# Position terms of the attention scores: one 120-row bfloat16 matmul per head, or two in the head's own half of the rows

## The chip, the core and the metric

The kernel runs on one core of a Trainium2 chip. Its metric is the device time of one launch in microseconds (us). A core has a matrix engine (TensorE, PE in the profile; its weight loads are a row of their own, PEld), a vector engine (DVE), an activation engine (ACT), a general engine (POOL, GpSimd) and a queue engine that issues most DMAs (SP). SBUF and PSUM have 128 partitions[...].

## What is computed

The whole program is a transformer block with attention, followed by three spectral and scan layers on a 48 x 48 grid of tokens with 768 channels. Only the attention matters here: 12 heads of 64 channels, T = 2304 queries and as many keys.

```python
attn = jnp.einsum('bqc,bkc->bqk', q * scale, k)
rel_h = jnp.einsum('bhwc,hkc->bhwk', r_q, Rh)
rel_w = jnp.einsum('bhwc,wkc->bhwk', r_q, Rw)
attn = (attn.reshape(B * nh, H, W, H, W) + rel_h[:, :, :, :, None] + rel_w[:, :, :, None, :]).reshape(B * nh, H * W, H * W)
attn = jax.nn.softmax(attn, axis=-1)
out = jnp.einsum('bqk,bkc->bqc', attn, v)
```

A score is thus the product of query and key plus two position terms: one depends on the query and the key's row of the grid, one on the query and the key's column.

## The kernel before

The qkv phase writes q, k, v to DRAM, and the position terms too: `rw_d` and `rh_d` hold, for each query and each head, 48 column terms and 48 row terms. Each float32 term is kept as a sum of three bfloat16 parts, so that three bfloat16 products with a 0/1 table give back the float32 value nearly whole.

`attention_bounded` then works on pairs of heads (6), chunks of 464 queries (5, the last of 448) and tiles of 128 keys (18). The tile's keys are 8 rows by 16 columns of the grid. A list `work` cuts the 18 key tiles of a chunk into items of KB = 3, which gives 6 x 5 x 6 = 180 items. The scores are kept transposed, keys on partitions and queries along the free dimension; a tile of both heads fills two PSUM banks, and there are three such buffers.

For each item the program issues, in this order:

- `products` (line 576) for the three key tiles: per head one float32 matmul of keys by queries. Head 0 has its 64 channels in partitions 0 to 63, head 1 in 64 to 127. The hardware's records show each float32 matmul as two, each with its own weight load.
- `scores` (line 585) for the same three tiles: per head one bfloat16 matmul that adds the position terms to the same PSUM tile. Its weights are a 0/1 table `oneh` of 120 rows; its moving operand `bt` has 120 rows for the head: 3 parts x 16 columns, and 3 parts x 24 rows of the grid. The 48 grid rows are cut into two halves of 24, and the key's columns into KJ = 3 groups of 16, so `bt` is held for 2 x 3 cases and both heads. Then comes the exponential on ACT (line 587) into a float32 tile `p`, and the sum over key tiles on DVE (lines 592 and 595).
- `values` (line 606) for the three tiles of the item before: per head one float32 matmul of 64 output columns, accumulated over the chunk. Behind a chunk's last scores come its `row_sums` (line 614), the reciprocal (line 616), and, after the values, the final product (line 622).

The engines run their instructions in program order; only SP's and POOL's side work is placed between them by the scheduler. Two sets of query and bias tiles alternate by chunk: `load_chunk` is called at the start of a chunk for the next one and calls `load_bias` once per head (lines 505 and 506, four DMAs per head and per segment; a chunk that crosses a multiple of 768 queries has two segments). The `p` tiles come from a pool of ten. The same pool serves as the gate of `weight_sums`, a side stream that, once every six items, loads blocks of the projection and MLP weights (lines 776 and 796), combines them on POOL (lines 131 to 142) and stores them back (lines 780 and 802). All its DMAs go through the SP queue too. `load_ahead` loads the first chunk and the 0/1 table during the qkv phase.

`attention_any` is a second branch for scores out of bounds. It doesn't run with these inputs.

Of the kernel before, what the change touches and what calls it, by code (L numbers as in the profile page):

```python
# [12 lines left out]
F32 = mybir.dt.float32  # L13
BF16 = mybir.dt.bfloat16
# [6 lines left out]
P = 128  # L21
# [5 lines left out]
NH, HD = 12, 64  # L27
FF = 4 * C
NF = FF // P
TB = 384  # L30
NTB = T // TB
QB = 464
NQB = -(-T // QB)
LN_EPS = 1e-5
KTH, KTW = 8, 16
KJ = G // KTW
NBR = 3 * (KTW + G // 2)
# [469 lines left out]
        at += m  # L507


def queries(qc):  # L510

    return slice(qc * QB, min(T, (qc + 1) * QB))


def load_onehot(nc, pool, oneh_d, o):

    f = pool.tile([P, 3, P], F32, tag="onehf", name="onehf")
    nc.sync.dma_start(f[:NBR], oneh_d)
    nc.vector.tensor_copy(o[:NBR], f[:NBR])


def attention_loads(nc, q_d, k_d, v_d, rw_d, rh_d):

    def keys_values(kv, pr):
        nc.sync.dma_start(kv[:, :T], k_d[pr * P : (pr + 1) * P, :])
        nc.sync.dma_start(kv[:, T:].rearrange("p (t c) -> p t c", t=NT), v_d[:, :, pr * P : (pr + 1) * P])

    def chunk(qb, c):  # L530
        pr, qc = c
        q = queries(qc)
        n = q.stop - q.start
        nc.sync.dma_start(qb[0][:, :n], q_d[pr * P : (pr + 1) * P, q])
        for s in range(2):
            load_bias(nc, qb[1][:, s, :, :, :n], rw_d, rh_d, 2 * pr + s, q.start, n)

    return keys_values, chunk


def attention_bounded(tc, ahead, oT, beside, load_next):

    nc = tc.nc
    KB = 3
    (load_keys_values, load_chunk), kvs, qbs, ones, oneh = ahead
    with (
        tc.tile_pool(name="at_p", bufs=10) as pp,
        tc.tile_pool(name="at_r", bufs=2) as rp,
        tc.tile_pool(name="at_o", bufs=2) as op,
        tc.tile_pool(name="at_ps", bufs=3, space=PSUM) as ps_s,  # L560
        tc.tile_pool(name="at_pv", bufs=1, space=PSUM) as ps_v,
    ):
        keys = [kv[:, :T] for kv in kvs]
        vals = [kv[:, T:].rearrange("p (t c) -> p t c", t=NT) for kv in kvs]

        probs, scs = {}, {}
        size = lambda c: queries(c[1]).stop - queries(c[1]).start
        held = lambda c: qbs[(c[0] * NQB + c[1]) % 2]

        def products(c, kt):  # L570
            pr, qc = c
            n = size(c)
            ps = ps_s.tile([P, 2, 512], F32, tag="s", name=f"s_{pr}_{qc}_{kt}")
            for s in range(2):
                rows = slice(s * HD, (s + 1) * HD)
                nc.tensor.matmul(ps[:, s, :n], lhsT=keys[pr % 2][rows, kt * P : (kt + 1) * P], rhs=held(c)[0][rows, :n], start=True, stop=False)  # L576
            scs[c, kt] = ps

        def scores(c, kt):
            pr, qc = c  # L580
            n = size(c)
            b, j = divmod(kt, KJ)
            ps = scs.pop((c, kt))
            for s in range(2):
                nc.tensor.matmul(ps[:, s, :n], lhsT=oneh[:NBR, b % 3, :], rhs=held(c)[1][:NBR, s, b // 3, j, :n], start=False, stop=True)  # L585
            p = pp.tile([P, 2, QB], F32, tag="p", name=f"p_{pr}_{qc}_{kt}")[:, :, :n]
            nc.scalar.activation(p, ps[:, :, :n], AF.Exp)  # L587
            probs[c, kt] = p

            if kt == 1:  # L590
                acc = rp.tile([P, 2, QB], F32, tag="acc", name=f"acc_{pr}_{qc}")[:, :, :n]
                nc.vector.tensor_tensor(acc, probs[c, 0], p, ALU.add)
                probs[c] = acc
            elif kt > 1:
                nc.vector.tensor_tensor(probs[c], probs[c], p, ALU.add)  # L595

        avs, recs = {}, {}

        def values(c, kt):
            pr, qc = c  # L600
            if kt == 0:
                avs[c] = ps_v.tile([P, 512], F32, tag="av", name=f"av_{pr}_{qc}")
            p = probs.pop((c, kt))
            for s in range(2):
                rows = slice(s * HD, (s + 1) * HD)
                nc.tensor.matmul(avs[c][rows, : size(c)], lhsT=vals[pr % 2][:, kt, rows], rhs=p[:, s, :], start=kt == 0, stop=kt == NT - 1)  # L606

        def row_sums(c):
            pr, qc = c
            n = size(c)  # L610
            acc = probs.pop(c)
            rs = ps_v.tile([P, 512], F32, tag="rs", name=f"rs_{pr}_{qc}")
            for s in range(2):
                nc.tensor.matmul(rs[s * HD : (s + 1) * HD, :n], lhsT=ones, rhs=acc[:, s, :], start=True, stop=True)  # L614
            rec = rp.tile([P, QB], F32, tag="rec", name=f"rec_{pr}_{qc}")[:, :n]
            nc.vector.reciprocal(rec, rs[:, :n])  # L616
            recs[c] = rec

        def finish(c):
            pr, qc = c  # L620
            av, rec = avs.pop(c), recs.pop(c)
            nc.vector.tensor_tensor(oT[:, pr, queries(qc)], av[:, : size(c)], rec, ALU.mult)

        work = [((pr, qc), k0) for pr in range(NC) for qc in range(NQB) for k0 in range(0, NT, KB)]
        other = beside(op, lambda name: pp.tile([P, 2, QB], F32, tag="p", name=name).rearrange("p a c -> p (a c)")[:, : 2 * TB].rearrange("p (a c) -> p a c", a=2))
        for i in range(len(work) + 1):
            if i % 6 == 3:
                next(other, None)
            if i == len(work) - 8:
                load_next()  # L630
            if i < len(work):
                c, k0 = work[i]
                pr, qc = c
                if k0 == 0:
                    nxt = (pr, qc + 1) if qc + 1 < NQB else (pr + 1, 0)
                    if nxt[0] < NC:
                        load_chunk(held(nxt), nxt)
                    if qc == 1 and pr + 1 < NC:
                        load_keys_values(kvs[(pr + 1) % 2], pr + 1)
                for kt in range(k0, k0 + KB):  # L640
                    products(c, kt)
                for kt in range(k0, k0 + KB):
                    scores(c, kt)
            if i:
                c, k0 = work[i - 1]
                if k0 + KB == NT:
                    row_sums(c)
                for kt in range(k0, k0 + KB):
                    values(c, kt)
                if k0 + KB == NT:  # L650
                    finish(c)
        for _ in other:
            pass


def attention_any(tc, ident, oneh, q_d, k_d, v_d, rw_d, rh_d, oT, beside, load_next):


    nc = tc.nc
# [6 lines left out]
    with (  # L666
# [7 lines left out]
    ):  # L674
        ones = cp.tile([1, HD], F32, tag="ones", name="an_ones")
        nc.vector.memset(ones, 1.0)
        ka = cp.tile([HD, T], F32, tag="ka", name="an_ka")
        vt = cp.tile([P, NT, HD + 1], F32, tag="vt", name="an_vt")
        nc.vector.memset(vt[:, :, HD : HD + 1], 1.0)
        for h in range(NH):  # L680
# [4 lines left out]
            bt = hp.tile([P, 2, KJ, T], BF16, tag="bt", name=f"an_bt_{h}")  # L685
            for i in range(NTB):
                load_bias(nc, bt[:, :, :, i * TB : (i + 1) * TB], rw_d, rh_d, h, i * TB, TB)
            for t in range(NT):
                s = sp.tile([P, T], F32, tag="s", name=f"an_s_{h}_{t}", bufs=1)
                m6 = sp.tile([P, T // TB], F32, tag="m6", name=f"an_m_{h}_{t}")  # L690
                for i in range(T // TB):
                    ps = ps_s.tile([P, 512], F32, tag="s", name=f"an_sp_{h}_{t}_{i}")
                    cols = slice(i * TB, (i + 1) * TB)
# [12 lines left out]
                for k0 in range(0, NT, 4):  # L706
                    n = min(4, NT - k0)
                    ps = ps_t.tile([P, 512], F32, tag="t", name=f"an_pt_{h}_{t}_{k0}")
                    for j in range(n):
                        k = k0 + j  # L710
# [600 lines left out]
def block_kernel(ctx: ExitStack, tc: tile.TileContext, a: dict):  # L1311
    nc = tc.nc
# [16 lines left out]
    loads = attention_loads(nc, q_d, k_d, v_d, rw_d, rh_d)  # L1329
    kvs, ahead = [], []  # L1330
    atc = at_stack.enter_context(tc.tile_pool(name="at_c", bufs=1, side="left"))
    oneh = atc.tile([P, 3, P], BF16, tag="oneh", name="oneh")

    def kv_tile():
        kvs.append(home.tile([P, 2 * T], F32, tag="xn", name=f"kv_{len(kvs)}"))

    def load_ahead(stage):
        if stage == 0:
            load_onehot(nc, atc, a["oneh"], oneh)
            kv_tile()  # L1340
            loads[0](kvs[0], 0)
            return
        kv_tile()
        pool = at_stack.enter_context(tc.tile_pool(name="at_a", bufs=1, side="left"))
        qbs = [(pool.tile([P, QB], F32, tag=f"qt{i}", name=f"qt{i}"), pool.tile([P, 2, 2, KJ, QB], BF16, tag=f"bt{i}", name=f"bt{i}")) for i in range(2)]
        loads[1](qbs[0], (0, 0))
        ones = pool.tile([P, HD], F32, tag="ones", name="ones")
        nc.vector.memset(ones, 1.0)
        ahead.extend((loads, kvs, qbs, ones, oneh))
# [16 lines left out]
    with tc.If(bounded > 0) as which:  # L1366
        attention_bounded(tc, ahead, oT, beside, load_pw)
    with which.Else():
        attention_any(tc, ident, oneh, q_d, k_d, v_d, rw_d, rh_d, oT, beside, load_pw)
    at_stack.close()  # L1370
    xr_d = dram.tile([T, C], F32, tag="xr_d", name="xr_d")
    proj_phase(tc, x, pw, ps_d, a["proj_b"], oT, xr_d)
# [484 lines left out]
```

## Time and profile before

| quantity | value |
|---|---|
| median of 3 runs | 3815.2 us (3811.54 to 3820.01) |
| the profiled execution's own time | 3815.61 us |
| its span, first to last instruction | 3813.4 us |
| attention, from its first product to the end of the last values | about 512 to 1666 us |
| mean granted clock of TensorE | 0.987 |
| bytes moved by DMA | 460.28 MB |

Median durations of the rows that the change concerns:

| line | instruction | count | ns of one |
|---|---|---|---|
| L576 | matmul, keys by queries, float32 | 2160 | 549 |
| L576 | weight load 64x128, float32 | 2160 | 187 |
| L585 | matmul, position terms, bfloat16 | 1080 | 359 |
| L585 | weight load 120x128, bfloat16 | 1080 | 98 |
| L587 | exponential, both heads | 540 | 940 (mean) |
| L595 | sum over key tiles | 480 | 1170 (mean) |
| L606 | matmul, probabilities by values, float32 | 2160 | 557 (mean) |

A matmul's duration in the profile runs from its start to its modelled end, and neighbours overlap; what one costs in a stream is the distance from one start to the next. In a line of the timeline the columns are start, length, engine, source line, operation, output and inputs, shapes and count; in square brackets stands idle time before it and what ended it.

### The profile page before, as it was taken

The page shows a single profiled execution, that of the slowest core. Times are in us where ns is not written, and L with a number is a line of the kernel's source. Part 1 is how long each engine was busy: PE and PEld are TensorE (multiplying, and loading weights), DVE is VectorE, ACT ScalarE, POOL GpSimd, SP SyncE. Part 2 cuts the span into 40 slices and gives each one's busy share as a digit, 9 for nine tenths or more (in the row PEclk, how much of TensorE's full clock was granted, in tenths as well). Part 3 has the DMA queues.
Part 4 walks back from the last instruction along what each step waited for, and adds up shares of the span by engine and source line. Part 5 has one row for each costly group of instructions (what it writes and reads, how often), then busy time and mean ns, then how long its engine had stood idle before and what let it go on. Part 6 is the DMA issues. An engine that isn't in the chain of part 4 may idle for free.

```text
span 3813.4 us, 51839 instructions
## 1 busy us (share of the span) xinstructions
PE 3707.4 (97%) x20914; PEld 2168.0 (57%) x20914; DVE 2032.0 (53%) x3070; ACT 1135.3 (30%) x1803; POOL 653.5 (17%) x498
## 2 busy tenths in 40 slices
PE   7999979999999999998999999999999998999998
PEld 4666543333333333345555555555568876996685
DVE  6655455656566666565424433232325567995455
ACT  1323244444444444420310120011013356222342
POOL 3101001111111111025000000000013301981131
PEclk9999989999999999999999999999999999999999
DMA  7655563333332322124334534443454402112345
GB/s 261 209 191 190 182 189 121 114 108 114 102 101 90 101 90 76 50 86 156 133 105 134 172 109 126 134 133 108 125 161 110 112 29 94 40 33 73 98 117 154
DMA packets 276271, 460.28 MB, mean 121 GB/s; under 512 B 50909, under 2 KB 228821, under 8 KB 269527
## 3 DMA queue, kind: packets, MB, share of 16 engines
q1 hardware_dynamic: 266215, 435.94, 37.5%
q10 hardware_dynamic: 9808, 20.94, 1.5%
q8 instruction: 167, 2.74, 0.3%
q14 instruction: 81, 0.66, 0.1%
HBM read 318.49 MB, written 138.31 MB: 120 GB/s over the span
## 4 chain that ended last, share of the span: by engine, by line
PE 87%; DVE 4%; POOL 3%; DMA 3%; ACT 1%; issue 1%; SPq 0%; ACTq 0%; POOLq 0%; DVEq 0%
PE p L886 13%; PE p L949 13%; PE s L576 12%; PE av L606 11%; PE qk L297 6%; PE s L585 6%; PE c L1113 4%; PE v L166 3%; POOL t L1214 2%; PE pj L166 2%; PE f_z L1516 2%; PE f_z L1517 2%; PE f_x L1481 2%; PE so L1291 2%; PE f_u L1531 2%; PE rh L417 1%
## 5 line engine op out<-in xcount | busy, mean ns | idle before, releaser
L595 DVE TENSOR_TENSOR acc<-acc,p 128x928 f32<-128x928 f32 (+1 forms) x480 | 561.6, 1170 | 359.4 <-ACT p L587 328.1
L587 ACT ACTIVATE p<-s 128x928 f32<-128x928 f32 (+1 forms) x540 | 467.9, 940 | 681.5 <-PE s L585 575.1
L949 PE MATMUL p<-w,h 128*128 128x384 f32 x1512 | 492.7, 486 | 0.0
L576 PE MATMUL s<-qt,kv 64*128 64x464 f32 (+1 forms) x2160 | 467.8, 565 | 7.6 <-ACT p L587 5.4
L606 PE MATMUL av<-p,kv 128*64 128x464 f32 (+1 forms) x2160 | 456.3, 557 | 0.0
L949 PEld LDWEIGHTS p<-w,h 128*128 128x128 f32 x1512 | 286.2, 190 | 196.9
L576 PEld LDWEIGHTS s<-qt,kv 64*128 64x128 f32 x2160 | 194.2, 187 | 277.5 <-issue 161.9
L886 PE MATMUL p<-x2nT,w 128*128 128x384 f32 x864 | 293.9, 490 | 3.3 <-issue 3.3
L606 PEld LDWEIGHTS av<-p,kv 128*64 128x64 f32 x2160 | 141.9, 136 | 247.1 <-issue 237.8
L297 PE MATMUL qk<-xnT,wqk 128*128 128x384 f32 x756 | 252.5, 491 | 5.0 <-DMA wqk<-wqk_d 5.0
L1206 PE MATMUL c<-H,bands 128*48 128x96 f32 x5632 | 243.8, 247 | 11.4 <-issue 10.9
L1206 PEld LDWEIGHTS c<-H,bands 128*48 128x48 f32 x5632 | 234.8, 123 | 20.6 <-issue 11.3
L585 PE MATMUL s<-bt,oneh 120*128 120x464 bf16 (+1 forms) x1080 | 241.3, 359 | 0.0
L886 PEld LDWEIGHTS p<-x2nT,w 128*128 128x128 f32 x864 | 165.4, 192 | 119.2 <-issue 6.1
L886 PE MATMUL p<-xT,w 128*128 128x384 f32 x648 | 220.8, 486 | 0.0
L297 PEld LDWEIGHTS qk<-xnT,wqk 128*128 128x128 f32 x756 | 144.6, 193 | 99.8 <-issue 8.3
L585 PEld LDWEIGHTS <-oneh 120*128 120x128 bf16 x1080 | 90.9, 98 | 190.8 <-issue 110.3
L925 POOL TENSOR_TENSOR rr<-rr,ml_b 128x1152 f32<-128x1152 f32 x12 | 31.5, 2622 | 955.6 <-DMA rr<-xr_d 863.6
L881 ACT ACTIVATE h<-h,ml_b 128x384 f32<-128x384 f32 x144 | 88.3, 614 | 346.6 <-DVE h L901 174.3
L1214 POOL TENSOR_TENSOR t<-s,c 128x768 f32<-128x768 f32 x80 | 144.5, 1832 | 179.5 <-DMA bands<-in_bands_dram 168.9
L886 PEld LDWEIGHTS p<-xT,w 128*128 128x128 f32 x648 | 123.1, 190 | 85.9
L616 DVE RECIPROCAL rec<-rs 128x464 f32<-128x464 f32 (+1 forms) x30 | 91.1, 3038 | 98.7 <-PE rs L614 98.7
(322 smaller groups left out, 4792.6 us busy)
## 6 DMA issues: line engine op xcount, KB each, us to landing
w<-w1s_d SPq DMA_DIRECT2D x36, 768.0 KB
w<-w2s_d SPq DMA_DIRECT2D x36, 768.0 KB
w<-w1s_d SPq DMA_DIRECT2D x36, 576.0 KB
w<-in_mlp_w_dram SPq DMA_DIRECT2D x27, 768.0 KB
wqk<-wqk_d SPq DMA_DIRECT2D x12, 1344.0 KB
yu<-f_ys SPq DMA_DIRECT2D x24, 672.0 KB
f_yt<-yu SPq DMA_DIRECT2D x20, 720.0 KB
yu<-f_us SPq DMA_DIRECT2D x18, 720.0 KB
```

The source lines that it names most:

```text
L166: nc.tensor.matmul(p[:, :TB], lhsT=rhs[n][:, c, t * P : (t + 1) * P], rhs=w[:, c, :], start=c == 0, stop=c == NC2 - 1)
L297: nc.tensor.matmul(p[:, :TB], lhsT=w[:, n, c, :], rhs=ops[sb][n][:, c, :], start=c == 0, stop=c == NC2 - 1)
L576: nc.tensor.matmul(ps[:, s, :n], lhsT=keys[pr % 2][rows, kt * P : (kt + 1) * P], rhs=held(c)[0][rows, :n], start=True, stop=False)
L585: nc.tensor.matmul(ps[:, s, :n], lhsT=oneh[:NBR, b % 3, :], rhs=held(c)[1][:NBR, s, b // 3, j, :n], start=False, stop=True)
L587: nc.scalar.activation(p, ps[:, :, :n], AF.Exp)
L595: nc.vector.tensor_tensor(probs[c], probs[c], p, ALU.add)
L606: nc.tensor.matmul(avs[c][rows, : size(c)], lhsT=vals[pr % 2][:, kt, rows], rhs=p[:, s, :], start=kt == 0, stop=kt == NT - 1)
L886: nc.tensor.matmul(p[:, :TB], lhsT=w[n][:, c, :], rhs=rhs[n][:, c, :], start=c == 0, stop=c == NC2 - 1)
L949: nc.tensor.matmul(ps[t][:, :TB], lhsT=hs[left, f][:, t * P : (t + 1) * P], rhs=wt[:, f % KW2, :], start=f == 0, stop=f == NF2 - 1)
L1113: nc.tensor.matmul(ps[:K, i, :n], lhsT=v[:, c, tok : tok + K], rhs=w[:, cc, c0 : c0 + n], start=cc == NC - 1, stop=cc == 0)
L1206: nc.tensor.matmul(ps[r0 : r0 + G, k // 4, cols], lhsT=bands[:, n - GC, i, :] if gr else bands0[:, n, i, :], rhs=H[:, n, :, d : d + NPR], ...
L1214: GP.tensor_tensor(t, sc[:, ch], c1[:, m0 : m0 + GC].unsqueeze(2).to_broadcast([P, GC, RR, NPR]), ALU.mult)
```

## The change

The position terms of head s now lie in partitions 64 s to 64 s + 63. The 120 rows of a head are cut in two: a first pass of 64 rows (48 column rows and the first 16 of the 72 row terms) and a second of 56 rows. `scores` issues four matmuls per key tile instead of two, pass by pass, and the heads alternate within a pass. The tile `bt` has 2 x 3 cases for the first pass and 2 for the second, since the second holds row terms only, which don't depend on the column group; `load_bias_halves` fills it, with ten DMAs per segment for both heads together. The 0/1 table is cut in the same way and loaded for both halves. And the item's loop is changed: the scores of a key tile are issued right behind the products of that tile, where the three tiles' products used to come first.

```diff
+def load_bias_halves(nc, bt, rw_d, rh_d, c, t0, n):
+    nw = 3 * KTW
+    at = t0
+    while at < t0 + n:
+        sb, t = divmod(at, 2 * TB)
+        m = min(2 * TB - t, t0 + n - at)
+        cols = slice(2 * c * TB + t, 2 * c * TB + t + m)
+        dst = bt[:, :, at - t0 : at - t0 + m]
+        for s in range(2):
+            w = rw_d[s].rearrange("(j k) n b f -> j (k n) b f", j=KJ)[:, :, sb, cols].rearrange("j r t -> r j t")
+            r = rh_d[s].rearrange("(a k) n b f -> a (k n) b f", a=2)[:, :, sb, cols]
+            p0 = s * HD
+            for a in range(2):
+                nc.sync.dma_start(dst[p0 : p0 + nw, a * KJ : (a + 1) * KJ], w)
+                nc.sync.dma_start(dst[p0 + nw : p0 + HD, a * KJ : (a + 1) * KJ], r[a, : HD - nw].unsqueeze(1).to_broadcast([HD - nw, KJ, m]))
+            nc.sync.dma_start(dst[p0 : p0 + NBR - HD, 2 * KJ :], r[:, HD - nw :].rearrange("a r t -> r a t"))
+        at += m
...
+def load_onehot_halves(nc, pool, oneh_d, o):
+    f = pool.tile([P, 2, 3, P], F32, tag="onehf", name="onehf")
+    for s in range(2):
+        p0 = s * HD
+        nc.sync.dma_start(f[p0 : p0 + HD, 0], oneh_d[:HD])
+        nc.sync.dma_start(f[p0 : p0 + NBR - HD, 1], oneh_d[HD:])
+        nc.vector.tensor_copy(o[p0 : p0 + HD, 0], f[p0 : p0 + HD, 0])
+        nc.vector.tensor_copy(o[p0 : p0 + NBR - HD, 1], f[p0 : p0 + NBR - HD, 1])
...
         nc.sync.dma_start(qb[0][:, :n], q_d[pr * P : (pr + 1) * P, q])
-        for s in range(2):
-            load_bias(nc, qb[1][:, s, :, :, :n], rw_d, rh_d, 2 * pr + s, q.start, n)
+        load_bias_halves(nc, qb[1][:, :, :n], rw_d, rh_d, pr, q.start, n)
...
-            for s in range(2):
-                nc.tensor.matmul(ps[:, s, :n], lhsT=oneh[:NBR, b % 3, :], rhs=held(c)[1][:NBR, s, b // 3, j, :n], start=False, stop=True)
+            for k in range(2):
+                for s in range(2):
+                    rows = slice(s * HD, s * HD + (NBR - HD if k else HD))
+                    rhs = held(c)[1][rows, 2 * KJ + b // 3 if k else b // 3 * KJ + j, :n]
+                    nc.tensor.matmul(ps[:, s, :n], lhsT=oneh[rows, k, b % 3, :], rhs=rhs, start=False, stop=k == 1)
...
                 for kt in range(k0, k0 + KB):
                     products(c, kt)
-                for kt in range(k0, k0 + KB):
                     scores(c, kt)
...
-    oneh = atc.tile([P, 3, P], BF16, tag="oneh", name="oneh")
+    oneh = atc.tile([P, 2, 3, P], BF16, tag="oneh", name="oneh")
...
-            load_onehot(nc, atc, a["oneh"], oneh)
+            load_onehot_halves(nc, atc, a["oneh"], oneh)
...
-        qbs = [(pool.tile([P, QB], F32, tag=f"qt{i}", name=f"qt{i}"), pool.tile([P, 2, 2, KJ, QB], BF16, tag=f"bt{i}", name=f"bt{i}")) for i in range(2)]
+        qbs = [(pool.tile([P, QB], F32, tag=f"qt{i}", name=f"qt{i}"), pool.tile([P, 2 * KJ + 2, QB], BF16, tag=f"bt{i}", name=f"bt{i}")) for i in range(2)]
```

The other branch, `attention_any`, loads a table of its own in the old form.

More of the change, by code (lines that the diff above doesn't have):

```diff
@@ L653, in attention_bounded, with attention_any @@
             pass
-def attention_any(tc, ident, oneh, q_d, k_d, v_d, rw_d, rh_d, oT, beside, load_next):
+def attention_any(tc, ident, oneh_d, q_d, k_d, v_d, rw_d, rh_d, oT, beside, load_next):
     nc = tc.nc
@@ L676, in attention_any @@
         nc.vector.memset(ones, 1.0)
+        oneh = cp.tile([P, 3, P], BF16, tag="oneh", name="an_oneh")
+        load_onehot(nc, cp, oneh_d, oneh)
         ka = cp.tile([HD, T], F32, tag="ka", name="an_ka")
@@ L1368, in block_kernel @@
     with which.Else():
-        attention_any(tc, ident, oneh, q_d, k_d, v_d, rw_d, rh_d, oT, beside, load_pw)
+        attention_any(tc, ident, a["oneh"], q_d, k_d, v_d, rw_d, rh_d, oT, beside, load_pw)
     at_stack.close()
```

## The prediction

> **What bounds the kernel now.** I read the page first (busy shares, chain), then the attention stretch as a window, its groups, and one period of its timeline engine by engine.
>
> ```profile
> span 3813.4 us, 51839 instructions
> PE 3707.4 (97%) x20914; PEld 2168.0 (57%) x20914; DVE 2032.0 (53%) x3070; ACT 1135.3 (30%) x1803; POOL 653.5 (17%) x498
> ...
> PE 87%; DVE 4%; POOL 3%; DMA 3%; ACT 1%; issue 1%; SPq 0%; ACTq 0%; POOLq 0%; DVEq 0%
> ```
>
> TensorE is busy 97% of the span and holds 87% of the chain. The same in the attention (from 512 us), and in one chunk of queries (the third):
>
> ```profile
> 512.00:1666.00 1154.00, 1147.95 (x5500) 431.42 (x5502) 691.40 (x569) 469.04 (x542) 139.18 (x108) 1.00 0.33 98
> ```
> ```profile
> 593.70:632.30 38.60, 38.60 (x186) 14.40 (x184) 23.10 (x20) 15.69 (x18) 5.37 (x4) 1.00 0.37 116
> ```
>
> Columns: stretch, length, then busy time of PE, weight loads, DVE, ACT, POOL, then PE clock, DMA share, GB/s. PE has no idle time; DVE (23.1 of 38.6) and ACT (15.7) have room. So time is won or lost here only by what PE spends. Yet a busy PE need not stream, so I look at one item of work, three key tiles:
>
> ```profile
> 1003.25 2.61 PE L576 MATMUL s<-qt,kv 64*128 64x464 f32 x12
> 1003.74 0.19 PEld L576 LDWEIGHTS s<-qt,kv 64*128 64x128 f32 x2 [0.20 <-issue]
> 1004.13 0.19 PEld L576 LDWEIGHTS s<-qt,kv 64*128 64x128 f32 x2 [0.20 <-issue]
> ...
> 1005.78 0.90 PEld L585 LDWEIGHTS <-oneh 120*128 120x128 bf16 x6 [0.68 <-issue]
> 1005.78 1.35 PE L585 MATMUL s<-bt,oneh 120*128 120x464 bf16 x6
> 1006.39 2.62 ACT L587 ACTIVATE p<-s 128x928 f32<-128x928 f32 x3 [3.69 <-PE s L585]
> ...
> 1007.06 2.56 PE L606 MATMUL av<-p,kv 128*64 128x464 f32 x12
> 1007.36 3.58 DVE L595 TENSOR_TENSOR acc<-acc,p 128x928 f32<-128x928 f32 x3 [2.11 <-ACT p L587]
> ...
> 1009.55 2.61 PE L576 MATMUL s<-qt,kv 64*128 64x464 f32 x12
> ```
>
> Start to start: products 2.53 us, scores 1.28, values 2.49: period 6.30. The products' loads come two at a time, 0.39 apart: the two heads sit in the two row halves and run together, one pair per 0.39. Values run in column-half pairs at the same pace. Six scores overlap with the last at 0.36 each, so they start (1.35-0.36)/5 = 0.198 apart, the first a little more; later ones are 0.195. Pure streaming is 6x0.389 + 6x0.195 + 6x0.389 = 5.84. The other 0.46 us lies at the three changes of shape (64x128, 120x128, 128x64). A narrow window shows the one that matters:
>
> ```profile
> 1004.91 0.94 PE L576 MATMUL s<-qt,kv 64*128 64x464 f32 x4
> 1005.78 0.37 PE L585 MATMUL s<-bt,oneh 120*128 120x464 bf16 x1
> ```
>
> The last product pair starts at 1004.91+0.39 = 1005.30, the first score at 1005.78: 0.49 instead of 0.39, so 0.10 lost, plus 0.01 in the first score's own spacing: **0.11 us**. Scores to values costs 0.145 (0.09 of gap, 0.05 in the first pair), values to products 0.205 (0.10 and 0.105); together 0.46, as above.
>
> **What the Trainium skill says.** TensorEngine Tiling (Array Packing), Key Properties: "Changing tiling mode (not just tile) drains the TensorE". The trace agrees: each change shows a 0.09 to 0.10 us gap, whether the element type changes with it or not (values to products is f32 to f32). Same page, Gotcha 1: different row tiles may not write one PSUM bank at once; each head has its own half of the 2x512 f32 tile, and the product pairs overlap so already. TensorE: Matmul & The Clock Gate, Part 3, gives 3.07x for four row tiles of K=32 at N=512; this trace shows two-row overlap only for f32. That part also says that a weight load overlaps running matmuls only in other row groups; the trace contradicts it, since the six 120-row loads run under the six 120-row scores.
>
> **The change, part by part.**
>
> *PE.* Per key tile, before: 8 f32 instructions in 4 products (2 pairs, 0.78) and 2 scores (0.39). After: the same 2 pairs, then 4 half-row bf16 scores, in the order head 0, head 1, head 0, head 1, so 2 pairs. If a pair takes one matmul's 0.195, that is 0.39 again: streaming is unchanged. The products-to-scores shape change disappears, because both now use 64-row halves (the second pass with 56 rows in the same half). Gain 0.11 us x 180 items (30 chunks x 6) = **20 us**. The other two changes stay. An item becomes 6.19. A bf16 pair at half rows reads per partition no more than an f32 pair does (464x2 bytes in 0.195 us against 464x4 in 0.389), which speaks for the overlap; the PSUM write rate is not shown.
>
> *Weight loads.* 2,160 small loads instead of 1,080, 0.098 each, two side by side under a 0.195 pair: hidden. Now an f32 load (0.187) must hide behind a bf16 pair (0.195) twice an item, where it had 0.389. It fits by 8 ns. If it did not, the values-to-products case shows 0.105 exposed: 2x0.105x180 = 38 us. I take 0.
> Issue: 8 instructions in 0.39 us is 49 ns each. The conv stage has 512 PE records starting 20.6 ns apart on average (near 3232 us), so issue does not bind.
>
> *Alternating f32 and bf16 in one shape.* Five new type changes an item (three to bf16, two back). Not shown by itself. Lower bound 0: a gap with a type change is no longer than one without. Upper: as costly as a shape change, 3x0.11+2x0.205 = 0.74. Below 0 is excluded: streaming cannot shrink. I take 0.
>
> *Waits.* A product now stands behind the previous tile's scores and waits for the exp three tiles back. From an item's start, the exps start at 0.78+0.195+0.36+0.04 = 1.37, 2.54 and 3.71, the last ending at 4.65; the next item's products come at 6.19, 7.36, 8.52: 3.9 us of slack. Behind such a wait the whole PE queue would stand; it never lasts. The row-sum reciprocal and the next chunk's values profit from earlier exps.
>
> *Exps come earlier, so their p buffers are asked for earlier.* Ten are shared with the weight-sum stream, which holds some until POOL or a store is done. In the first half POOL is done some 12 us ahead of the exp that takes the buffer. In the second half a store is issued near 1231.85 and another at 1235.53, and the first exp concerned now runs near 1237.4 rather than a tile later: slack about 3 us by my estimate. Cost 0; if a stall of 0.67 us came in each of 30 chunks, the gain would be gone.
>
> *DMA.* Each query segment takes 10 issues on SP instead of 8 (42 segments: 84 more, 0.40 us each, 34 us of SP in 1,134), but 992 rows instead of 1,440: 12.4 MB less. Loads go a chunk (38 us) ahead, and the DMA share is 0.37. They are felt only at the start: PE idles 3.65 us before 553.64, as an exp waits for POOL's pw0p, whose load is queued on SP behind the biases of chunk 1. Four more issues (+1.7) against 0.4 MB less (-1.8 at the 234 GB/s there): 0, between -2 and +2. The one-hot table costs three more loads and three more DVE copies (at most 0.55 each) beside qkv work: 0 to 2 us.
>
> *Sum*: 3813.4 - 20 = 3793.4 span. The profiled execution took 3815.61; the median is 3815.2; so **3795 us**.
>
> **Rivals.**
> 1. *Halves do not overlap in bf16.* Then each tile has 2x0.195 more: 0.39x540 = 210, less 20: about 4005. For: no bf16 row pair in the trace. Against: f32 pairs, the same read rate, the skill's figure. 9%.
> 2. *Type changes drain PE* (other side). At the full 0.74 an item: (0.74-0.11)x180 = +113, 3928; it decides from 22 ns per change on (0.11/5). The 38 us case of exposed f32 loads is its milder form (3833). For: only combined changes are seen. Against: the type adds nothing to a gap when both change. About 10% slower than 3823; 8% ends within the bound of no change, 4% around 3805.
> 3. *The gain is given back* by p buffers or SP: 3815 or a little more; 3%, split into the same and slower.
> 4. *The drain does not belong to the shape*: nothing changes, 3815; its chance is within the 8%.
>
> **Numbers.** Likeliest, 66%: 3795, own range 3790 to 3801. Faster by over 0.2% (7.6 us, about what a measurement of this kernel can tell from no change): 66+4 = 70%. Same: 8%. Slower: 22%. The range 3787 to 3832 holds the likeliest, the mild forms and no change; it leaves out rival 1 and most of rival 2.
>
> **What will show it.** Right: an item of 6.19 us; score halves start in pairs, 0.195 from pair to pair, and f32 pairs stay 0.39 apart inside an item; exps spread 1.17 apart; PE busy without gaps from the third chunk on. Wrong: scores at 0.195 singly (rival 1); 0.1 gaps between a tile's scores and the next products (rival 2); exps ended by POOL or DMA (rival 3). A faster result with changes between types that cost something would mean the same mechanism with a smaller size.

## The result, and the profile after

The changed kernel takes 3798.6 us (median of 6 runs, 3794.1 to 3803.0) against 3817.0 us (6 runs, 3811.5 to 3820.0) in the same session. The ratio is 0.9955 with a 95% interval of 0.9942 to 0.9968, so it is faster by 18 us, clear of no change. The forecast was 3795, in a range of 3787 to 3832. The profiled execution took 3803.02 us, the longest of the six, with a span of 3800.9.

The page of the changed kernel has the same picture as before, TensorE busy and on the chain:

```profile
span 3800.9 us, 54128 instructions
PE 3694.8 (97%) x21994; PEld 2188.4 (58%) x21994; DVE 2048.6 (54%) x3073; ACT 1174.1 (31%) x1803; POOL 667.8 (18%) x498
...
PE 87%; DVE 4%; DMA 3%; POOL 3%; ACT 2%; issue 1%; SPq 0%; ACTq 0%; POOLq 0%; DVEq 0%
```

So the gain has to lie in what PE spends on an item. One item of the changed kernel, from the timeline (line 607 is the products, 619 the scores, 621 the exps, 640 the values):

```profile
999.97 1.05 PE L607 MATMUL s<-qt,kv 64*128 64x464 f32 x4
1000.86 0.56 PE L619 MATMUL s<-bt,oneh 64*128 64x464 bf16 x4
1001.05 0.39 PEld L607 LDWEIGHTS s<-qt,kv 64*128 64x128 f32 x4
1001.25 0.94 PE L607 MATMUL s<-qt,kv 64*128 64x464 f32 x4
1001.45 0.94 ACT L621 ACTIVATE p<-s 128x928 f32<-128x928 f32 x1 [2.91 <-PE s L619]
...
1002.03 0.56 PE L619 MATMUL s<-bt,oneh 64*128 64x464 bf16 x4
1002.03 0.10 PEld L619 LDWEIGHTS <-oneh 56*128 56x128 bf16 x2 [0.29 <-issue]
...
1002.42 0.94 PE L607 MATMUL s<-qt,kv 64*128 64x464 f32 x4
1002.65 0.94 ACT L621 ACTIVATE p<-s 128x928 f32<-128x928 f32 x1 [0.26 <-PE s L619]
...
1003.21 0.56 PE L619 MATMUL s<-bt,oneh 64*128 64x464 bf16 x4
1003.69 2.56 PE L640 MATMUL av<-p,kv 128*64 128x464 f32 x12
...
1006.18 1.05 PE L607 MATMUL s<-qt,kv 64*128 64x464 f32 x4
```

An item is 6.21 us (999.97 to 1006.18) where it was 6.30. Four half-row scores take 1001.25 - 1000.86 = 0.39 us, the time of two full-row ones: the two halves run side by side. In the second tile, products start at 1001.25, scores at 1002.03: 0.78, exactly two float32 pairs, so the gap of 0.10 us into the scores, which the prediction read in the kernel before, is gone. The way back to the products shows none either: from 1002.03 to 1002.42 is 0.39. The float32 loads of the next tile run under the last pair of scores (1001.05, four loads under the matmuls of 1000.86 and 1001.25). The exps come one per tile, 1.2 us apart.

From about 600 us to the end of the attention PE has no idle time at all (busy 1055.00 of the 1055.00 us from 597 to 1652), but the start of chunk 1 holds a longer stop than before. The groups of ACT and PE around it, in the timeline of the kernel before:

```profile
552.64 2.62 ACT L587 ACTIVATE p<-s 128x928 f32<-128x928 f32 x3 [9.57 <-POOL pw0p L133]
553.64 4.11 PE L576 MATMUL s<-qt,kv 64*128 64x464 f32 x12 [3.65 <-ACT p L587]
```

and in that of the changed kernel:

```profile
555.32 2.62 ACT L621 ACTIVATE p<-s 128x928 f32<-128x928 f32 x3 [15.47 <-POOL pw0p L133]
556.32 1.92 PE L607 MATMUL s<-qt,kv 64*128 64x464 f32 x4 [8.76 <-ACT p L621]
```

An exp waits for a p tile that the side stream holds as `pw0b`: POOL reads it for the last time at line 133, and the exp starts as that ends. PE then waits for the exp, 8.76 us instead of 3.65, and runs slowly for a while (four products in 1.92 us instead of 1.05), as it does before (twelve in 4.11 instead of 2.61). The load of `pw0b`, for which POOL waits, stands on the changed kernel's chain (start, length):

```profile
546.89 6.07 DMA pw0b<-in_proj_w_dram
```

The projection behind the attention starts at 1657.40 us instead of 1672.02 in the two profiled executions (before, the last values end at about 1671, not at 1666 as the table ahead has it). These 14.6 us are made up as follows: the attention starts 0.2 us earlier; its first twelve items take 84.1 us instead of 81.1; the rest of it is 17.5 us shorter, nearly all of it 168 items of 0.096. Behind the attention the two executions differ by 2.1 us the other way.

### The profile page after: what moved, and what is told of

It reads as the page before. It is cut to its first block, busy times and chain, and to the rows that moved or that the text cites. A ratio compares the mean times of both kernels' runs of the same rounds, so it can differ in the third digit from the quotient of the medians.

```text
span 3800.9 us, 54128 instructions
## 1 busy us (share of the span) xinstructions
PE 3694.8 (97%) x21994; PEld 2188.4 (58%) x21994; DVE 2048.6 (54%) x3073; ACT 1174.1 (31%) x1803; POOL 667.8 (18%) x498
## 4 chain that ended last, share of the span: by engine, by line
PE 87%; DVE 4%; DMA 3%; POOL 3%; ACT 2%; issue 1%; SPq 0%; ACTq 0%; POOLq 0%; DVEq 0%
PE p L921 13%; PE p L984 13%; PE s L607 12%; PE av L640 12%; PE qk L297 6%; PE s L619 6%; PE c L1148 4%; PE v L166 3%; PE pj L166 2%; PE f_z L1551 2%; PE f_z L1552 2%; PE f_x L1516 2%; PE so L1326 2%; PE f_u L1566 2%; POOL t L1249 1%; PE rh L417 1%
## 5 line engine op out<-in xcount | busy, mean ns | idle before, releaser
L629 DVE TENSOR_TENSOR acc<-acc,p 128x928 f32<-128x928 f32 (+1 forms) x480 | 572.8, 1193 | 322.2 <-ACT p L621 288.2
L621 ACT ACTIVATE p<-s 128x928 f32<-128x928 f32 (+1 forms) x540 | 506.6, 939 | 630.5 <-PE s L619 614.1
L607 PE MATMUL s<-qt,kv 64*128 64x464 f32 (+1 forms) x2160 | 528.0, 565 | 10.6 <-ACT p L621 8.9
L619 PE MATMUL s<-bt,oneh 64*128 64x464 bf16 (+3 forms) x2160 | 301.4, 355 | 0.0
L619 PEld LDWEIGHTS <-oneh 64*128 64x128 bf16 (+1 forms) x2160 | 108.2, 93 | 260.5 <-issue 256.6
L166 PE MATMUL v<-wv,xnT 128*128 128x384 f32 x378 | 134.3, 501 | 0.6 <-DVE xnT L141 0.5
```

The lines of the kernel that those rows point to most:

```text
L166: nc.tensor.matmul(p[:, :TB], lhsT=rhs[n][:, c, t * P : (t + 1) * P], rhs=w[:, c, :], start=c == 0, stop=c == NC2 - 1)
L619: nc.tensor.matmul(ps[:, s, :n], lhsT=oneh[rows, k, b % 3, :], rhs=rhs, start=False, stop=k == 1)
```

## The experiments

**The order alone.** The kernel before, with each tile's full-row scores behind its products:

```diff
                 for kt in range(k0, k0 + KB):
                     products(c, kt)
-                for kt in range(k0, k0 + KB):
                     scores(c, kt)
```

> The kernel before with the loop order of the changed one alone: each key tile's 120-row scores right behind its products. Theory (PE drains at a change of shape): an item has two more changes into the scores (0.11 us each) and two more back to the products (about 0.205 each), so it takes 6.30 + 0.63 = 6.93 us and the launch 3817 + 113 = 3930 us. Rival (the gain comes from the order, through earlier exps): an item below 6.30 us and a launch below 3817 us. Rival (the gap belongs to the change of element type, not of shape): the same 3930 us, so this run doesn't tell shape from type; the next one does.

It took 3919.6 us (one run; before: 3817.0). Its timeline:

```profile
1003.03 1.05 PE L576 MATMUL s<-qt,kv 64*128 64x464 f32 x4
1004.01 0.57 PE L585 MATMUL s<-bt,oneh 120*128 120x464 bf16 x2
1004.51 1.05 PE L576 MATMUL s<-qt,kv 64*128 64x464 f32 x4
...
1007.46 1.00 PE L606 MATMUL av<-p,kv 128*64 128x464 f32 x4
```

A tile takes 1004.51 - 1003.03 = 1.48 us where its streaming is 1.17: the 0.3 lies in one change into the scores and one back. An item is 6.92 us (6.93 expected). 180 x 0.61 is 110 us; the launch is only 103 longer, mostly because the stop at chunk 1 does not occur here: a slower PE arrives later, when the p tile is free, and all its waits for exps come to 0.3 us. The order by itself is thus a loss with full-row scores, and changes of shape or of type, one of the two, cost what the forecast read from the trace.

**The halves alone.** The changed kernel with the loop order of before:

```diff
                 for kt in range(k0, k0 + KB):
                     products(c, kt)
+                for kt in range(k0, k0 + KB):
                     scores(c, kt)
```

> The changed kernel with the loop order of before: three tiles' products, then the half-row scores of all three. One change of element type from products to scores per item instead of three, no change of shape there. Theory (shape alone counts): the same as the changed kernel, 3797 to 3799 us, an item of 6.19 to 6.21 us. If alternating types is what makes the changed kernel's item 6.207 instead of the 6.192 forecast, the item here is 6.195. Rival (the order is needed for the gain): 6.30 us an item and 3817 us. Rival (a change of type drains): the gap of 0.10 us between products and scores is still there.

It took 3801.7 us, ratio 0.9957 (0.9941 to 0.9974), which is not told apart from the changed kernel's 0.9955. One item:

```profile
999.74 2.61 PE L607 MATMUL s<-qt,kv 64*128 64x464 f32 x12
1002.18 1.35 PE L619 MATMUL s<-bt,oneh 64*128 64x464 bf16 x12
1003.47 2.56 PE L640 MATMUL av<-p,kv 128*64 128x464 f32 x12
1005.95 2.22 PE L607 MATMUL s<-qt,kv 64*128 64x464 f32 x10
```

By the start times of single matmuls, which the trace keeps to the ns, the item is 6.209 us, with one change of element type inside the shape where the changed kernel has five and 6.207. So alternating float32 and bfloat16 in one shape costs nothing that an item shows, which settles that rival, and the gain of the steady items is that of the row halves; the order adds nothing to them. Once, at the second item of the attention, the order does help: there PE waits 1.7 us for an exp before, and about as long here, but 0.2 us in the changed kernel, whose exps come earlier. The last product pair ahead of the scores and the scores themselves:

```profile
1001.79 0.56 PE L607 MATMUL s<-qt,kv 64*128 64x464 f32 x2
1002.18 1.35 PE L619 MATMUL s<-bt,oneh 64*128 64x464 bf16 x12
```

0.39 from the last product pair to the first scores: no gap, though the type changes there. The start of the values at 1003.47 ends the six pairs after 1.29 us; single start times put them 0.198 apart on average, where the full-row scores stood 0.195 to 0.196 apart. A few ns a pair are thus most of the 15 ns by which the item is longer than forecast.

**Head by head.** Both passes of head 0, then both of head 1:

```diff
-            for k in range(2):
-                for s in range(2):
+            for s in range(2):
+                for k in range(2):
```

> The changed kernel with the four scores of a tile issued head by head (both passes of head 0, then both of head 1) instead of pass by pass. Theory (matmuls start in order, and two overlap only when neighbours lie in different row halves): the four take three slots of 0.195 us instead of two, an item 6.207 + 3 x 0.195 = 6.79 us, the launch 3799 + 105 = 3904 us. Rival (the overlap doesn't depend on the order of issue): an item of 6.21 us, 3799 us. Rival (the loads of the second pass stop the overlap altogether): 6.207 + 3 x 0.39 = 7.38 us, 4009 us.

It took 3803.7 us (one run), with an item of 6.207 us: the first expectation failed. Four half-row scores again take one pair's time twice:

```profile
1002.12 0.56 PE L619 MATMUL s<-bt,oneh 64*128 64x464 bf16 x4
```

Narrower windows take these four apart:

```profile
1002.12 0.36 PE L619 MATMUL s<-bt,oneh 64*128 64x464 bf16 x2
```
```profile
1002.31 0.36 PE L619 MATMUL s<-bt,oneh 56*128 56x464 bf16 x2
```

The first two matmuls have 64 rows and start within 10 ns of each other, the next two have 56 and start 0.195 us later, though the program now issues 64, 56, 64, 56 rows. So the second half's 64-row matmul starts ahead of the first half's 56-row one, which stands before it in the program: the rule given ahead, that an engine runs its instructions in program order, does not hold here between the two row halves.

**The price of the overlap.** Both heads from the same row half, so that head 1's own products and position terms are left out:

```diff
-                rows = slice(s * HD, (s + 1) * HD)
+                rows = slice(0, HD)
...
-                    rows = slice(s * HD, s * HD + (NBR - HD if k else HD))
+                    rows = slice(0, NBR - HD if k else HD)
```

> The changed kernel with both heads' products and scores taken from partitions 0 to 63, so that head 1 repeats head 0 (its own products and position terms are left out). The number and shapes of the instructions are the same; only the row half is. Theory (the second head rides in the free half at no cost): every pair becomes two slots, 4 x 0.389 + 4 x 0.195 = 2.34 us a tile instead of 1.17, an item 6.21 + 3.5 = 9.7 us, 3799 + 630 = 4429 us; the scores alone stand 0.195 apart one by one. Rival (the score halves never overlapped, or overlap within one half too): score starts unchanged.

It took 4429.8 us (one run), as expected to within 1 us.

```profile
1005.55 1.72 PE L607 MATMUL s<-qt,kv 64*128 64x464 f32 x4
1007.11 0.94 PE L619 MATMUL s<-bt,oneh 64*128 64x464 bf16 x4
1007.89 1.72 PE L607 MATMUL s<-qt,kv 64*128 64x464 f32 x4
```

A tile is 1007.89 - 1005.55 = 2.34 us, and its four scores take 0.78 instead of 0.39. The second head is free in the other half and costs a full matmul in the same one.

**The stop at chunk 1.** The side stream of weight sums begins six items later, in the changed kernel and in the kernel before:

```diff
-            if i % 6 == 3:
+            if i > 6 and i % 6 == 3:
```

> The changed kernel with the side stream of weight sums starting six items later (its first call at item 9 instead of 3, the last at 177 instead of 171). Theory (the stop of PE at the start of chunk 1 is an exp that waits for the p tile of pw0b, whose load stands on SP behind the biases): the stop of 8.8 us and the slow clock behind it are gone, the first twelve items take about 77 us instead of 84.1, and the launch about 3791 us. Rival (chunk 1's biases are themselves late): a stop of similar length stays, now ended by a bias DMA, and the time stays at 3799 us.

> The kernel before with the side stream starting six items later, as in e4_gate_later. Theory (the same stop at chunk 1, ended by the same p tile): 3.65 us of idle and about 1.5 us of slow clock go, 3811 us; set against e4_gate_later (3791) the change itself is then worth 20 us, as its steady items say (180 x 0.096 = 17 us). Rival (the stop belongs to the changed kernel's extra loads alone): 3817 us.

The changed kernel takes 3791.5 us, ratio 0.9935 (0.9919 to 0.9952), and its first twelve items 73.0 us instead of 84.1. PE's busy time in nearly the same stretch, of the changed kernel and of this one (columns as before: stretch, length, PE busy, ...):

```profile
512.50:596.60 84.10, 75.16 (x424) 29.97 (x424) 44.44 (x38) 35.12 (x38) 9.53 (x8) 0.94 0.57 162
```
```profile
509.50:585.50 76.00, 75.82 (x444) 30.59 (x445) 43.70 (x38) 36.52 (x40) 5.56 (x4) 1.00 0.57 155
```

9 us of idle and the clock of 0.94 are gone, without a change to the biases: it was the p tile, not chunk 1's own loads. (The second stretch is some 3 us longer than its first twelve items.) The kernel before takes 3812.8 us with the same edit, ratio 0.9991 (0.9982 to 1.0), which by itself is hardly clear of no change; its first twelve items take 75.9 us instead of 81.1. Without the stop on either side the change is worth 0.9935 against 0.9991, or some 21 us: 17 in the steady items (180 x 0.096), 1.5 by the shorter wait at the second item, and a rest within the scatter of the runs.

**Fewer changes of shape.** If a change of shape is what costs, the two that remain in each item can be halved. Items of six tiles, values right behind their own scores:

```diff
-    KB = 3
+    KB = 6
...
-            if i % 6 == 3:
+            if i % 3 == 1:
...
-            if i:
-                c, k0 = work[i - 1]
-                if k0 + KB == NT:
-                    row_sums(c)
                 for kt in range(k0, k0 + KB):
                     values(c, kt)
                 if k0 + KB == NT:
+                    row_sums(c)
                     finish(c)
```

> The changed kernel with items of six key tiles instead of three, each item's values right behind its own scores (no longer an item later), row sums behind the values, and the side stream called every third item. Streaming is the same; half of the remaining changes of shape go. Theory (a change costs 0.145 into the values and 0.205 out of them): 90 items less of 0.35 us, so 31 us less: 3768 us, an item of 12.06 us for six tiles instead of 12.41. Rival (the exps of the last tiles, or the ten p tiles, hold up the values or the next products): PE idles ended by ACT in every item, and the gain shrinks or turns into a loss; 0.35 us of idle per item is the point from which it does.

> Both together: items of six tiles and the side stream starting two of these items, a chunk's third, later. Theory (the two gains lie in different places and add): 3791 - 31 = 3760 us. Rival (the p tiles, now asked for sooner, are held by the side stream): idle before products ended by ACT, and no better than e5_six_tiles.

With the side stream as it was: 3761.5 us, ratio 0.9855 (0.9839 to 0.9872); with the later side stream (condition `i > 3 and i % 3 == 1`): 3759.2 us, 0.9851 (0.9834 to 0.9867). An item is 12.066 us in both (12.06 expected), against 2 x 6.207. One item of the second, and its PE over most of the attention:

```profile
1000.94 1.05 PE L607 MATMUL s<-qt,kv 64*128 64x464 f32 x4
...
1008.19 4.89 PE L640 MATMUL av<-p,kv 128*64 128x464 f32 x24
1013.01 1.05 PE L607 MATMUL s<-qt,kv 64*128 64x464 f32 x4
```

```profile
600.00:1590.00 990.00, 990.00 (x5932) 417.95 (x5930) 639.93 (x513) 454.91 (x486) 123.89 (x100) 1.00 0.29 89
```

90 items of 0.35 us less are 31 us; the first of the two runs gains 37, because its stop is shorter too. Its changed condition calls the side stream three key tiles earlier in a chunk, the load of `pw0b` is issued at 538.28 us instead of 546.89, the waiting exp starts at 548.25 instead of 555.32, and PE stops for only 2.8 and 1.6 us. So the later side stream has little left to bring here, 2 us by the medians, which is within their intervals.

Items of nine tiles, with `KB = 9`, thirteen p tiles and the condition `i > 2 and i % 2 == 1`:

> As e7_six_tiles_gate_later with items of nine key tiles, two per chunk, thirteen p tiles instead of ten, and the side stream called every second item from item 3 on. Theory (each pair of changes of shape into and out of the values costs 0.35 us): 30 pairs fewer, 10.5 us less: 3749 us, an item of 9 x 1.17 + 9 x 0.78 + 0.35 = 17.92 us. Rival (DVE's sums or the p tiles hold up values or row sums in long items): idle on PE ended by ACT or DVE in every chunk, and no better than 3759 us.

3750.2 us, ratio 0.9821 (0.9804 to 0.9837); an item is 17.923 us (17.92 expected). This is the fastest kernel of the study: about 69 us below the one before in its session, 48 below the changed one by two medians of different sessions.

## Why the prediction was right

- *Bound.* Right. PE is busy 97% of the span after as before, and in the attention from 600 us on it has no idle time. Nothing but PE's own work moved the steady state.
- *Scores in halves stream as fast as whole ones.* Right, to a few ns: the four take 0.39 us, and in one row half they take 0.78. This rival was given 9%; its price (0.39 a tile) is what the run in one half shows. The argument from the equal read rate cannot be told apart from others by these runs; that the overlap exists is shown.
- *The lost change of shape, 0.11 us an item.* Right in kind, 0.096 in size. The 0.10 gap and the 0.01 are gone, but the forecast gave the halves exactly the pace of whole scores: by single start times a tile's second pair takes 0.200 us instead of 0.195, and the product pair behind it 0.392 instead of 0.389, which takes 15 ns of each item back. 180 x 0.096 = 17 us instead of 20.
- *Type changes at nothing.* Right, by the pair of orders (6.207 and 6.209 us). The 0 was a choice between two bounds, not a reading, so this term had some luck. Only the run with the old order separates shape from type; the trace of before and the order-only run could not.
- *Float32 loads under a 0.195 us pair.* Right: no gap of the kind feared (0.105 us) ahead of the products within an item. The few ns more in the pairs don't come from these loads, nor from the alternation of types: in the old order only bfloat16 loads run under the half-row pairs, and the pairs stand 0.198 apart all the same. Where these ns come from stays open.
- *p tiles in the later chunks, SP's 84 further issues.* Right: no idle time there.
- *The start: 0, between -2 and +2.* This step failed. The first twelve items lost 3.0 us where the steady gain would have been 1.2, a cost of 4.2. The two queue lines of SP show why, before and after:

```profile
544.88 0.43 SPq L776 DMA_DIRECT2D pw0b<-in_proj_w_dram  x1
```
```profile
546.89 0.44 SPq L811 DMA_DIRECT2D pw0b<-in_proj_w_dram  x1
```

The load is issued 2.0 us later, and POOL starts on it 6.5 us after its issue instead of 5.8, so the exp comes 2.7 us later. I had set 1.7 us for four more issues against 1.8 for the smaller bytes; nothing came back for the smaller bytes. And I had left out that a quicker PE reaches the wait earlier: its values ahead of the stop start at 545.00 instead of 547.43. What is gained ahead of a fixed event is lost at it, so the stop grows by both, about 5 us. Starting the side stream later removes it.
- *The sum.* In the profiled executions: 0.2 by the earlier start, 3.0 lost in the first twelve items, 17.5 gained in the rest, 2.1 lost behind the attention, which makes the span 12.5 us shorter. The medians differ by 18, between 12 and 22 by the interval. The profiles account for less than that, and the runs scatter by some 9 us from lowest to highest, so that the median came within 4 us of the forecast is in part luck: the mechanism is shown by the item, not by the launch.
- *Two slips that change nothing.* The mild form at 3833 us lies 1 us above the range that is said to hold it, and the 22% for slower count all 3% of the third rival, which the text splits.

## What to carry to other kernels

On a saturated TensorE, read the distance from start to start, not the busy share. Here what exceeded streaming sat where the tile shape changes, and splitting a matmul over the row halves of its neighbours removed such a change at the cost of 15 ns an item. Before reordering, count the changes of shape per period and lengthen the runs between them; here six tiles in place of three took 31 us from the items, and the split 17. And when a faster engine meets a wait for a fixed event, such as a buffer behind a loaded DMA queue, look whether that event can be moved.

## What was not expected of the hardware

- Two row halves follow their own order of instructions: with the program's order 64, 56, 64, 56 rows over halves 0, 0, 1, 1, the 64-row matmuls still start within 10 ns of each other and the item stays at 6.207 us. The Trainium skill (TensorE: Matmul & The Clock Gate, Part 3) says that matmuls start strictly in program order; this run shows otherwise for matmuls in different row halves.
- Half-row bfloat16 pairs of 464 columns stand 0.198 us apart on average when they follow each other, full-row matmuls 0.195 to 0.196.
